# Attention with a fourth-power score and a mixture of experts: when relu buffers are given back, and a new set of order weights

## The chip, the cores and the metric

The kernel runs on one core of one Trainium2 chip. The metric is the time of one execution on the device in microseconds (us), the median over several executions. The core has five engines that work side by side, each through its own queue of instructions: TensorE (PE, matmuls; PEld is its weight loads), VectorE (DVE), ScalarE (ACT), GpSimd (POOL) and SyncE (SP, which here issues transfers). An engine takes the instructions of its queue in the order in which the program issued them.

## What is computed

A block over x of 4 batches, 1024 tokens and 128 channels. The normed input goes through an attention with 16 heads of 8 channels and through 8 experts of which each token takes 2; both results are added to x.

```python
xn = _layernorm(x)
# attention, per batch and head
s = einsum('td,sd->ts', q, k)
s = s - s.mean(-1); mad = abs(s).mean(-1) + 1e-6
s = where(causal, s / mad * score_gain, -1000.0)
r = maximum(s, 0.0) ** 4
att = r / (r.sum(-1) + 1e-6)
y = att @ v
# experts, per token, the two best of 8 with softmax weights
z = (xn @ w1[e] + b1[e]) * (xn @ w2[e] + b2[e])
out += weight * (silu(z @ wg[e] + bg[e]) @ w3[e] + b3[e])
x = x + attention + experts
```

The softmax is replaced by a relu to the fourth power, so a score is squared twice. The mean of the absolute scores is needed as well, over all tokens and not the causal ones alone.

## The kernel before

The program first describes its work as nodes and then has a planner put them in order. A node (`Plan.add`) has a name, the engines that could run it with a duration for each, the nodes that it depends on, the buffers that it takes and those that it gives back. `Plan.run` simulates the engines: again and again it looks at all nodes whose dependencies are met, and for each at every engine that could run it, computes the start that the engine and the buffers allow, and takes the node with the smallest key. The key is

```python
sooner = self.SOONER.get(n.name, 0.0) + self.SOONER.get(f"{n.name}@{e}", 0.0)
key = (s - sooner, n.rank + self.RANK.get(n.name, 0.0), s + took)
```

So `SOONER` holds a bonus in us for a name, and for a name on one engine; `RANK` only parts nodes whose first part of the key is equal. Instructions are then issued in order of the planned starts. That order is what each engine's queue has on the chip; waits between engines come from semaphores that follow the data, not from the planned times. Buffers are numbered slots of a kind, picked by the planner.

Attention is done in chunks: for each of 4 batches two chunks of 512 queries. Names carry a "0" in the first batch's two chunks (stage 0: `sq0`, `mask0`, `abs0` and so on) and a "2" in the last chunk. Heads come in 4 rounds (r) of 4, whose matmuls run in four quarters of the array at once. In a round:

- "up" (L1010) makes scores of queries against all keys that the causal part doesn't cover into 4 PSUM banks; "abs" sums their absolute values, on VectorE (L1023) or ScalarE (L1025), and gives the banks back.
- "score" (L1134) makes scores of a group of keys, transposed, into 4 banks. It also takes two relu buffers, `u1s`, of which there are 6 in all, enough for three groups.
- "mask" (L1153, VectorE) and "relu" (L1160 on ScalarE, L1162 on VectorE) move the scores into the relu buffers and free the banks.
- "sq" squares twice, on ScalarE (L1185) or POOL (L1187): the first squares (`sq1`) read the relu buffer and write a buffer `u`, the second (`e2`) work in place in `u`.
- "av" is a burst of two jobs (`flush`): the sums of relus (L1201, which read the relu buffers `u1`) and the values (L1210, which read `u`), both into one accumulator bank.
- "ys", "turn" (L1078) and "normal" evacuate, transpose and divide; "yT", "wT" and "proj" (L1267, L1269, L1279) project a whole chunk.

There are 8 PSUM banks for all of this. For each batch, "k", "q", "kappa", "bound", "keys", "blocks" and "heads" prepare the keys and queries.

Routing goes once over all batches: "top" finds the two best experts of each token, "count" and "place" (six nodes on VectorE, L663 to L703) give each token a slot in an expert's list, "weight" and "gates" the weights. Then POOL scatters the normed rows to their slots in DRAM with 64 indirect transfers ("scatter", L776). Before each eight of them "second" (L767) writes the weights into the rows. When all rows have been scattered, 36 tiles of experts run: "rows_in" and "load" (SP), "xg" (L1331), "h" (L1342, and L1360 of the tile before), "g" (L1351), "y", and "give" (L1380), an indirect transfer of POOL that adds the results in DRAM. At the end those sums are loaded back ("sums"), added on POOL ("sum", L1486) and stored.

The planner also pads: where TensorE would idle it adds matmuls with zeros (L1531, L1536).

Of the kernel before, what the change touches and what calls it, by code (L numbers as in the profile page):

```python
# [52 lines left out]
class Plan:  # L53
# [3 lines left out]
    HOP = 0.12  # L57
    LAG = {"PE": 0.2, "DVE": 0.085, "ACT": 0.1, "POOL": 0.045}

    SOONER = {"score": 0.46, "sum": -0.74, "mean": 0.17, "wT@DVE": 0.13, "norm@ACT": -0.05, "place": 0.03, "sums": 0.22, "relu0": -0.21, "relu2": -0.08, "score0": 0.74, "score2": 0.58, "sq2": 0.1, "ys0": -0.42, "out": -0.17, "v": -0.03, "gain": -0.81, "absq": 0.38, "abs0": -0.55, "sq0": -0.35, "proj": -0.44, "xT": 0.07, "second": -0.98, "up2": 0.18, "yT": 0.14, "up": 0.32, "sq@ACT": -0.27, "tbias": -0.01, "mask0": 0.04, "up0": 0.3, "abs0@DVE": 0.57, "ys2": -0.14, "ys@DVE": -0.79, "sq@POOL": -0.64, "weight": -0.19, "gate@ACT": -0.71, "count": 0.31, "k": 0.27, "turn": -0.06, "xT@ACT": 0.41, "y@DVE": 0.14, "gateT": 0.32, "abs2@DVE": 0.08, "gate": 0.05, "scatter": -0.07, "heads@ACT": 0.06, "abs@DVE": -0.3, "exp": 0.12, "xT@DVE": -0.16, "moments": -0.1, "keys": -0.69, "heads@DVE": 0.12, "relu0@ACT": -0.27, "rows": -0.52, "av0": -0.04, "scale": 0.09, "sq2@ACT": -0.42, "xg": -0.43, "av2": 0.03, "ys": 0.07, "abs2": 0.05, "warm": -0.75, "bias": -0.8, "gates": 0.91, "std": 0.14, "ys@ACT": -0.12, "sq0@ACT": -0.2, "q@ACT": 0.05, "ys2@ACT": -0.68, "mask": -0.04, "q": 0.08, "bound@DVE": -0.04, "norm": 0.17, "y": 0.11, "yT@DVE": -0.66, "norm@DVE": -0.66, "ys0@ACT": 0.07, "give": 0.2, "sq0@POOL": 0.01, "yT@ACT": -0.42, "headsT": 0.91, "abs2@ACT": -0.01, "blocks": -0.07, "sq": -0.1, "rows_in": -0.92, "xg@ACT": 0.35, "h": 0.17, "relu@DVE": -0.2, "load": 0.26, "xg@DVE": -0.07, "bound": 0.03, "abs": 0.51, "spill": -0.52, "kappa": 0.65, "relu2@DVE": -0.07, "relu": 0.05}  # L60
    RANK = {"xg": -16, "headsT": 6, "spill": 168, "blocks": 174, "wT": 8, "absq": 58, "abs": 20, "weight": 101, "gain": 188, "keys": -227, "abs2": 39, "sq2": 19, "ys0": -9, "up0": -37, "score2": 1, "av": -8, "second": 1, "score0": 14, "relu2": 94, "heads": -7, "norm": 28, "abs0": -107, "h": 174, "sums": 228, "av0": 17, "xT": -7, "relu": -11, "stats": -9, "rows_in": -149, "gateT": -21, "sq": 161, "top": 102, "reload": 84, "ys2": 27, "k": 242, "up": 10, "hot": -130, "score": -18, "sum": 13, "mean": 156, "kappa": -33, "load": -208, "warm": 37, "ys": -195, "yT": 1, "turn": -123, "rows": -17, "av2": 1, "out": 6, "normal": 62, "proj": -184, "scale": 29, "fill": 13, "mask2": 35, "sq0": -53, "tbias": -32, "count": 13, "gates": 7, "std": 24, "up2": -6, "gate": 6, "bias": 6, "mask0": -13, "v": 14, "scatter": 1, "g": 53, "moments": -184}
    MODE = {"up": "rows", "score": "rows", "av": "columns", "gate": "columns", "heads": "columns"}

    @classmethod
# [13 lines left out]
    def add(self, name, on, emit, deps=(), take=(), give=(), rank=0.0, after=0.0, begin=0.0,  # L78
            behind=()):
        n = Node(name, on, emit, deps, list(take), list(give), rank, after, begin, behind)  # L80
        self.nodes.append(n)
        return n

    def run(self):
# [9 lines left out]
        while len(order) < len(self.nodes):  # L94
            best = None
            for n in ready:
# [81 lines left out]
def layer_kernel(  # L178
# [63 lines left out]
    def keep(shape, name, dtype=F32):  # L242
        return const.tile(shape, dtype, name=name)
# [16 lines left out]
    add = plan.add  # L260
# [11 lines left out]
    rows = keep([3, P], "rows")  # L272
# [8 lines left out]
    gain = keep([P, 1], "gain")  # L281
# [14 lines left out]
    for r in range(NR):  # L296
        for g in range(4):
            h = g * NR + r
# [20 lines left out]
    for base, step in ((0, -D), (D - 1, D)):  # L319
        nc.gpsimd.affine_select(  # L320
            out=same.rearrange("p (h d) -> p h d", d=D), in_=same.rearrange("p (h d) -> p h d", d=D),
# [7 lines left out]
        out=causal[:, : 2 * P].rearrange("p (n k) -> p n k", k=P), in_=causal[:, : 2 * P].rearrange("p (n k) -> p n k", k=P),  # L329
# [3 lines left out]
    for i in range(kinds["V"][0]):  # L333
        v = keep([P, TB, VW], f"V_{i}")
# [11 lines left out]
        out=behind_, in_=behind_, compare_op=ALU.is_ge, fill=0.0,  # L346
# [53 lines left out]
    none = tiles["w"][0][:, FILL * WX : FILL * WX + 2 * C]  # L400
# [43 lines left out]
    hot = [keep([P, E, NTB], f"hot_{k}") for k in range(2)]  # L444
# [350 lines left out]
    q, km, Vb, sh, prepared, keyed = {}, {}, {}, {}, {}, {}  # L795
# [190 lines left out]
    def chunk(b, c, vd, sh_done, t0, t1):  # L986
# [10 lines left out]
        for n, (r, unit) in enumerate(work):  # L997
# [20 lines left out]
            for g, k in enumerate(ks_):  # L1018
                def drain(e, r=r, parts=parts, g=g, k=k):
                    for i, sg, _, w, at in parts:  # L1020
# [9 lines left out]
                        deps=[a], behind=drained[0][:1], take=[] if drained[0] else [asum], give=[k], rank=rank - 200,  # L1030
# [15 lines left out]
        def flush(jobs, rank):  # L1046

            n = add(
                "av" + stage, {"PE": sum(o["took"] for o in jobs)}, lambda e: [o["emit"](e) for o in jobs],
                deps=[d for o in jobs for d in o["deps"]] + chain, take=[t for o in jobs for t in o["take"]],  # L1050
                give=[u for o in jobs for u in o["give"]], rank=rank - 20,
                behind=line["turn"][-2:-1] if any(o["take"] for o in jobs) else [],
            )
            chain[:] = [n]
            for o in jobs:
                if o["last"]:
                    n.closed = o["acc"]
                else:
                    n.open = o["acc"]
            for o in jobs:  # L1060
                if o["free"]:
                    u1s, e2 = o["free"]
                    add("free", {"none": 0.0}, None, deps=[n] + e2, give=u1s)
                if o["last"]:
                    finish(*o["last"], n, rank)

# [46 lines left out]
        for r in range(NR):  # L1113
            acc = Buf("bank")
            for j, grp in enumerate(groups):
                diag = grp[0][0] >= c * CB
# [9 lines left out]
                e1, e2, sq1 = [], [], []  # L1126
                u1s, us = ([Buf(kind) for _ in range(2)] for kind in ("u1", "u"))
# [17 lines left out]
                for m in range(2):  # L1145
                    u1, u = u1s[m], us[m]
                    a = []
                    for g in range(2):
                        k = ks_[2 * m + g]
# [20 lines left out]
                        if rest:  # L1170
# [3 lines left out]
                                    give=[] if near else [k], rank=rank - 200,  # L1174
# [31 lines left out]
                def values(e, r=r, parts=parts, us=us, acc=acc, begin=False, end=False):  # L1206
# [11 lines left out]
                begin, last = j == 0, j == jn - 1  # L1218
                relu_job = dict(
                    acc=acc,  # L1220
                    emit=lambda e, f=relus, s=begin and not diag: f(e, begin=s), deps=e1, took=took(counted), give=[],
                    free=(u1s, e2), last=None, take=[acc] if begin and not diag else [],
                )
                av_job = dict(
                    acc=acc,
                    emit=lambda e, f=values, s=begin and diag, t=last: f(e, begin=s, end=t), deps=e2 + vd, took=took(w),
                    give=us, free=None, last=(r, acc) if last else None, take=[acc] if begin and diag else [],
                )
                if begin and diag:
# [17 lines left out]
        k, yT = Buf("bank"), Buf("yT")  # L1247
# [7 lines left out]
        kw, wT = Buf("bank"), Buf("wT")  # L1255
# [10 lines left out]
        def project(e):  # L1266
# [15 lines left out]
            deps=[a] + first, give=[ko], rank=rank - 200,  # L1282
# [246 lines left out]
    for n in plan.run():  # L1529
# [4 lines left out]
        if n.pad:  # L1534
            acc, count = n.pad
# [33 lines left out]
```

## Time and profile before

| What | Before |
|---|---|
| median of 14 runs | 896.28 us (895.79 to 898.2) |
| the profiled execution | 896.33 us, of which the span of instructions 894.6 us |
| granted TensorE clock | 0.997 |
| scatter (L776), first and last start | 73.2 and 242.9 us |
| squares on POOL (L1187) | 302, 524.0 us |
| squares on ScalarE (L1185) | 338, 325.1 us |
| sums of absolute values on VectorE (L1023) | 417, 203.3 us |
| the same on ScalarE (L1025) | 351, 170.7 us |
| relus on ScalarE (L1160) and VectorE (L1162) | 353, 152.7 us and 159, 99.3 us |

Times of one instruction are averages over the profiled execution. A busy engine is one that has an instruction in it; for TensorE this includes matmuls that are drawn long since they wait for the one ahead.

```profile
L1187 POOL TENSOR_TENSOR u<-u 128x1024 f32<-128x1024 f32 (+1 forms) x302 | 524.0, 1832 | 93.4 <-ACT u L1160 47.3
L1185 ACT ACTIVATE u<-u 128x1024 f32<-128x1024 f32 (+1 forms) x338 | 325.1, 992 | 7.4 <-DVE u L1162 3.1
```

These are two of the page's costliest groups: line, engine, operation, what is written and read with its shape, how many; then busy us and mean ns of one; then the engine's idle time before them and what ended most of it.

### The profile page before, as it was taken

How to read it: one execution, taken by the hardware profiler on the slowest of the kernel's cores; microseconds unless marked ns; L12 is line 12 of the kernel's file. 1: busy time of each engine (PE TensorE's matmuls, PEld its weight loads, DVE VectorE, ACT ScalarE, POOL GpSimd, SP SyncE). 2: the span in 40 equal slices, each digit the busy share in tenths (PEclk: the TensorE clock that was granted, in tenths of full speed). 3: DMA queues.
4: the chain of work that ended last, by engine and by line, in shares of the span. 5: the costliest groups of instructions: out<-in, count | busy, mean ns of one | idle time of the engine just before them, and what ended most of it. 6: DMA issues, size and time to landing. Idle time of an engine off the chain costs nothing.

```text
span 894.6 us, 22584 instructions
## 1 busy us (share of the span) xinstructions
PE 875.9 (98%) x8067; PEld 469.5 (52%) x8067; DVE 593.3 (66%) x1557; ACT 787.1 (88%) x1881; POOL 710.4 (79%) x563
## 2 busy tenths in 40 slices
PE   7999999999999999999999999999999999999997
PEld 5455433334555555555566665555545666544444
DVE  6998967687865655554666666555756775755555
ACT  4978999999996999899988989989988978889995
POOL 5378998999995978787667839889787568599998
PEclk9999999999999999999999999999999999999999
DMA  4852001000001454535444534444213444422115
GB/s 112 311 153 86 25 26 32 31 13 25 26 20 49 101 128 91 127 77 144 94 111 105 134 92 120 96 122 117 72 52 73 104 111 107 108 72 54 23 15 186
DMA packets 92318, 79.20 MB, mean 89 GB/s; under 512 B 8431, under 2 KB 88366, under 8 KB 92206
## 3 DMA queue, kind: packets, MB, share of 16 engines
q1 hardware_dynamic: 79064, 68.50, 26.1%
q0 software_dynamic: 12416, 8.99, 7.3%
q8 instruction: 64, 1.05, 0.5%
q10 hardware_dynamic: 726, 0.27, 0.1%
q14 instruction: 48, 0.39, 0.1%
HBM read 58.13 MB, written 19.60 MB: 87 GB/s over the span
## 4 chain that ended last, share of the span: by engine, by line
PE 79%; ACT 6%; POOL 6%; DVE 5%; issue 2%; DMA 0%; DVEq 0%; POOLq 0%; ACTq 0%
PE bank L1010 16%; PE bank L1134 14%; PE bank L1210 14%; PE bank L1201 10%; PE bank L1351 7%; PE bank L1342 7%; PE bank L1360 4%; POOL u L1187 3%; ACT u L1185 2%; POOL xs L776 2%; ACT u L1160 2%; PE bank L1078 1%; DVE u L1153 1%; DVE asum L1023 1%; PE bank L1531 1%
## 5 line engine op out<-in xcount | busy, mean ns | idle before, releaser
L1187 POOL TENSOR_TENSOR u<-u 128x1024 f32<-128x1024 f32 (+1 forms) x302 | 524.0, 1832 | 93.4 <-ACT u L1160 47.3
L1185 ACT ACTIVATE u<-u 128x1024 f32<-128x1024 f32 (+1 forms) x338 | 325.1, 992 | 7.4 <-DVE u L1162 3.1
L1023 DVE TENSOR_REDUCE asum<-bank 128x1 f32<-128x512 f32 (+3 forms) x417 | 203.3, 547 | 71.3 <-PE bank L1010 70.1
L1025 ACT ACTIVATE bank<-bank 128x512 f32<-128x512 f32 (+3 forms) x351 | 170.7, 488 | 33.8 <-PE bank L1010 31.0
L1010 PE MATMUL bank<-blk,blk 32*128 32x512 f32 (+3 forms) x1536 | 181.2, 521 | 1.6 <-ACT s L1452 1.6
L1160 ACT ACTIVATE u<-bank 128x256 f32<-128x256 f32 (+2 forms) x353 | 152.7, 496 | 34.1 <-PE bank L1134 17.8
L1134 PE MATMUL bank<-blk,blk 32*128 32x512 f32 (+3 forms) x1536 | 178.4, 525 | 1.2 <-ACT blk L908 0.7
L1153 DVE SCALAR_TENSOR_TENSOR u<-bank,causal 128x256 f32<-128x256 f32 (+1 forms) x384 | 121.2, 373 | 74.4 <-PE bank L1134 37.7
L1380 POOL DMA_INDIRECT acc<-ye,xg x72 | 113.4, 1575 | 67.5 <-DVE ye L1372 39.3
L1210 PE MATMUL bank<-u,V 128*32 128x512 f32 (+3 forms) x1536 | 159.2, 497 | 0.1
L1162 DVE TENSOR_SCALAR u<-bank 128x512 f32<-128x512 f32 (+1 forms) x159 | 99.3, 660 | 50.1 <-PE bank L1134 50.0
L1010 PEld LDWEIGHTS bank<-blk,blk 32*128 32x128 f32 x1536 | 86.1, 183 | 80.3 <-DVE asum L1023 14.0
L1201 PE MATMUL bank<-u,pick 128*32 128x512 f32 (+3 forms) x1280 | 125.4, 469 | 0.0
L1134 PEld LDWEIGHTS bank<-blk,blk 32*128 32x128 f32 x1536 | 65.6, 183 | 64.5 <-issue 25.6
L1201 PEld LDWEIGHTS bank<-u,pick 128*32 128x32 f32 x1280 | 42.3, 111 | 80.3 <-issue 75.6
L1210 PEld LDWEIGHTS bank<-u,V 128*32 128x32 f32 x1536 | 32.8, 108 | 88.3 <-issue 67.3
L1351 PEld LDWEIGHTS bank<-z,w 128*128 128x128 f32 x576 | 67.2, 192 | 18.4 <-issue 5.9
L1426 DVE SCALAR_TENSOR_TENSOR z<-bank,biases,z 128x128 f32<-128x128 f32 x144 | 43.6, 345 | 46.2 <-ACT z L1419 45.6
L776 POOL DMA_INDIRECT xs<-blk,slot x64 | 62.9, 982 | 13.4 <-issue 10.7
L1351 PE MATMUL bank<-z,w 128*128 128x128 f32 x576 | 73.3, 280 | 0.0
L1342 PE MATMUL bank<-xT,w 128*128 128x128 f32 x576 | 70.3, 275 | 0.0
L1025 ACT ACTIVATION_READ_ACCUMULATOR bank<-bank 128x1 f32 x351 | 68.3, 195 | 0.0
(191 smaller groups left out, 724.3 us busy)
## 6 DMA issues: line engine op xcount, KB each, us to landing
w<-in_L_ffn_w_dram SPq DMA_DIRECT2D x216, 128.0 KB
w<-in_L_ffn_wg_dram SPq DMA_DIRECT2D x72, 256.0 KB
xs<-w SPq DMA_DIRECT2D x1, 4680.0 KB
xg<-xs SPq DMA_DIRECT2D x36, 130.0 KB
acc<-w SPq DMA_DIRECT2D x1, 2048.0 KB
blk<-acc SPq DMA_DIRECT2D x4, 512.0 KB
out_dram<-xt SPq DMA_DIRECT2D x8, 256.0 KB
xt<-in_L_attn_x_dram SPq DMA_DIRECT2D x3, 512.0 KB
```

The costliest lines, as they stand in the source:

```text
L1010: nc.tensor.matmul(of_buf(ks_[g])[:, at : at + w], of_buf(q[b])[rows_, ii * P : (ii + 1) * P], of_buf(km[b][r])[rows_, k0 : k0 + w], start ...
L1023: nc.vector.tensor_reduce(to, of_, AX.X, ALU.add, apply_absolute_value=True)
L1025: nc.scalar.activation(of_, of_, AF.Abs, accum_out=to)
L1134: nc.tensor.matmul(of_buf(ks_[g])[:, at : at + n], of_buf(km[b][r])[rows_, jj * P : (jj + 1) * P], of_buf(q[b])[rows_, c * CH + off : (c + ...
L1153: nc.vector.scalar_tensor_tensor(of_buf(u1)[:, g, :near], of_buf(k)[:, :near], 0.0, allowed[:, :near], ALU.max, ALU.mult)
L1160: nc.scalar.activation(to, s_, AF.Relu)
L1185: nc.scalar.activation(to, s_, AF.Square)
L1187: (nc.vector if e == "DVE" else nc.gpsimd).tensor_tensor(to, s_, s_, ALU.mult)
L1201: nc.tensor.matmul(of_buf(acc)[32 * g : 32 * g + 32, off + lo : CH], pick, of_buf(u1s[g // 2])[:, g % 2, at + lo : at + n], start=begin, s ...
L1210: nc.tensor.matmul(of_buf(acc)[32 * g : 32 * g + 32, off:CH], of_buf(Vb[b])[:, jj, h0 : h0 + 32], of_buf(us[g // 2])[:, g % 2, at : at + n ...
L1342: nc.tensor.matmul(of_buf(k)[:, m * TW + j * TS : m * TW + (j + 1) * TS], weights_of(i, j)[m][:, f * P : (f + 1) * P], of_buf(tile_[i]["xT ...
L1351: nc.tensor.matmul(of_buf(k)[:, g * TW + j * TS : g * TW + (j + 1) * TS], weights_of(i, j)[2][:, f, g * P : (g + 1) * P], of_buf(tile_[i][ ...
```

## The change

Two things. The relu buffers of a group are given back, in the plan, once the sums of relus and the first squares of the group are done, where before it was the sums of relus and the second squares. And both tables of weights for the order, `SOONER` and `RANK`, are replaced.

```diff
             for o in jobs:
                 if o["free"]:
-                    u1s, e2 = o["free"]
-                    add("free", {"none": 0.0}, None, deps=[n] + e2, give=u1s)
+                    u1s, squared = o["free"]
+                    add("free", {"none": 0.0}, None, deps=[n] + squared, give=u1s)
...
-                    free=(u1s, e2), last=None, take=[acc] if begin and not diag else [],
+                    free=(u1s, sq1), last=None, take=[acc] if begin and not diag else [],
...
                     if not counted:
-                        add("free", {"none": 0.0}, None, deps=e2, give=u1s)
+                        add("free", {"none": 0.0}, None, deps=sq1, give=u1s)
```

Of the tables, the bonuses of the names that the text speaks of, in us; on an engine the bonus of the name and that of the name on the engine add up, and what is not in the table is 0:

| Node, engine | before | after |
|---|---|---|
| score, up, av on PE | 0.46, 0.32, 0 | 0.41, 0.06, -0.20 |
| second, scatter on POOL | -0.98, -0.07 | 0.75, -0.18 |
| sq0 on POOL, on ACT | -0.34, -0.55 | 0, 0.01 |
| sq on POOL, on ACT | -0.74, -0.37 | -0.79, -0.48 |
| place, mask0, abs0 on DVE | 0.03, 0.04, 0.02 | -0.66, 0, 0.05 |
| mask on DVE | -0.04 | 0.66 |
| relu on DVE, on ACT | -0.15, 0.05 | 0.63, -0.01 |
| abs on DVE, on ACT | 0.21, 0.51 | 0, 0.10 |
| give on POOL | 0.20 | -0.12 |

More of the change, by code (lines that the diff above doesn't have):

```diff
@@ L58 @@
     LAG = {"PE": 0.2, "DVE": 0.085, "ACT": 0.1, "POOL": 0.045}
-    SOONER = {"score": 0.46, "sum": -0.74, "mean": 0.17, "wT@DVE": 0.13, "norm@ACT": -0.05, "place": 0.03, "sums": 0.22, "relu0": -0.21, "relu2": -0.08, "score0": 0.74, "score2": 0.58, "sq2": 0.1, "ys0": -0.42, "out": -0.17, "v": -0.03, "gain": -0.81, "absq": 0.38, "abs0": -0.55, "sq0": -0.35, "proj": -0.44, "xT": 0.07, "second": -0.98, "up2": 0.18, "yT": 0.14, "up": 0.32, "sq@ACT": -0.27, "tbias": -0.01, "mask0": 0.04, "up0": 0.3, "abs0@DVE": 0.57, "ys2": -0.14, "ys@DVE": -0.79, "sq@POOL": -0.64, "weight": -0.19, "gate@ACT": -0.71, "count": 0.31, "k": 0.27, "turn": -0.06, "xT@ACT": 0.41, "y@DVE": 0.14, "gateT": 0.32, "abs2@DVE": 0.08, "gate": 0.05, "scatter": -0.07, "heads@ACT": 0.06, "abs@DVE": -0.3, "exp": 0.12, "xT@DVE": -0.16, "moments": -0.1, "keys": -0.69, "heads@DVE": 0.12, "relu0@ACT": -0.27, "rows": -0.52, "av0": -0.04, "scale": 0.09, "sq2@ACT": -0.42, "xg": -0.43, "av2": 0.03, "ys": 0.07, "abs2": 0.05, "warm": -0.75, "bias": -0.8, "gates": 0.91, "std": 0.14, "ys@ACT": -0.12, "sq0@ACT": -0.2, "q@ACT": 0.05, "ys2@ACT": -0.68, "mask": -0.04, "q": 0.08, "bound@DVE": -0.04, "norm": 0.17, "y": 0.11, "yT@DVE": -0.66, "norm@DVE": -0.66, "ys0@ACT": 0.07, "give": 0.2, "sq0@POOL": 0.01, "yT@ACT": -0.42, "headsT": 0.91, "abs2@ACT": -0.01, "blocks": -0.07, "sq": -0.1, "rows_in": -0.92, "xg@ACT": 0.35, "h": 0.17, "relu@DVE": -0.2, "load": 0.26, "xg@DVE": -0.07, "bound": 0.03, "abs": 0.51, "spill": -0.52, "kappa": 0.65, "relu2@DVE": -0.07, "relu": 0.05}
@@ L61 @@
-    RANK = {"xg": -16, "headsT": 6, "spill": 168, "blocks": 174, "wT": 8, "absq": 58, "abs": 20, "weight": 101, "gain": 188, "keys": -227, "abs2": 39, "sq2": 19, "ys0": -9, "up0": -37, "score2": 1, "av": -8, "second": 1, "score0": 14, "relu2": 94, "heads": -7, "norm": 28, "abs0": -107, "h": 174, "sums": 228, "av0": 17, "xT": -7, "relu": -11, "stats": -9, "rows_in": -149, "gateT": -21, "sq": 161, "top": 102, "reload": 84, "ys2": 27, "k": 242, "up": 10, "hot": -130, "score": -18, "sum": 13, "mean": 156, "kappa": -33, "load": -208, "warm": 37, "ys": -195, "yT": 1, "turn": -123, "rows": -17, "av2": 1, "out": 6, "normal": 62, "proj": -184, "scale": 29, "fill": 13, "mask2": 35, "sq0": -53, "tbias": -32, "count": 13, "gates": 7, "std": 24, "up2": -6, "gate": 6, "bias": 6, "mask0": -13, "v": 14, "scatter": 1, "g": 53, "moments": -184}
+    SOONER = {"score": 0.41, "sum": -0.51, "mean": -1.23, "wT@DVE": 0.99, "norm@ACT": 0.12, "place": -0.66, "sums": 0.17, "gate@DVE": 0.09, "relu2": 0.33, "score0": 0.51, "score2": 0.47, "sq2": -0.62, "ys0": -0.74, "v": -0.26, "gain": 0.49, "absq": -0.12, "abs0": 0.05, "proj": -0.53, "xT": 0.08, "second": 0.75, "up2": 0.09, "yT": -0.55, "bound@ACT": 0.29, "relu@ACT": 0.14, "up": 0.06, "relu0@DVE": -0.5, "sq@ACT": -0.23, "tbias": 0.18, "up0": 0.49, "ys2": 0.2, "ys@DVE": 0.59, "sq@POOL": -0.54, "weight": 0.38, "gate@ACT": -0.35, "count": 0.4, "hot": 0.76, "k": 0.39, "turn": -0.14, "xT@ACT": 0.3, "fill": -0.49, "y@DVE": 0.62, "gateT": 0.03, "abs2@DVE": -0.61, "gate": -0.02, "scatter": -0.18, "heads@ACT": -0.17, "exp": 0.13, "moments": -0.51, "keys": -0.46, "heads@DVE": -0.08, "rows": 1.24, "av0": -0.17, "g": -0.13, "top": 0.31, "wT": -0.12, "scale": 0.35, "sq2@ACT": 0.16, "xg": -0.17, "av2": -0.1, "ys": -0.38, "abs2": 1, "warm": -0.06, "normal": -0.04, "heads": -0.22, "std": 0.18, "ys@ACT": 0.37, "sq0@ACT": 0.01, "q@ACT": -1.78, "ys2@ACT": 0.5, "abs0@ACT": 0.04, "mask": 0.66, "q": 0.07, "bound@DVE": 0.76, "yT@DVE": 0.13, "norm@DVE": -0.32, "ys0@ACT": 1.68, "give": -0.12, "blocks": -1.24, "abs@ACT": 0.1, "sq2@POOL": 0.26, "relu": -0.15, "yT@ACT": -0.1, "abs2@ACT": -0.69, "relu2@ACT": -0.05, "load": 0.31, "rows_in": 1.06, "ys2@DVE": 0.42, "xg@ACT": 0.02, "relu2@DVE": -0.13, "av": -0.2, "bound": -0.14, "relu@DVE": 0.78, "kappa": 0.42, "h": 0.02, "spill": 0.26, "sq": -0.25}
@@ new lines @@
+    RANK = {"xg": -15, "headsT": 25, "spill": 10, "blocks": -9, "y": 188, "exp": -1, "abs": 15, "weight": -238, "keys": 23, "abs2": 27, "relu0": -28, "sq2": 20, "ys0": -28, "up0": 66, "score2": -20, "av": -242, "second": 2, "score0": 11, "relu2": -156, "heads": -79, "place": -25, "norm": -9, "abs0": 24, "h": -14, "sums": -92, "av0": -11, "xT": 26, "rows_in": 7, "q": -2, "bound": -1, "sq": 21, "top": -71, "ys2": -97, "k": -11, "up": -16, "hot": -1, "score": -19, "sum": -28, "mean": 87, "kappa": -6, "give": 192, "load": 22, "ys": 17, "yT": 223, "turn": 34, "rows": -7, "av2": 227, "mask": -188, "out": 130, "scale": 4, "fill": 23, "mask2": -181, "sq0": -37, "bias": -154, "up2": 199, "mask0": 7, "scatter": 13, "moments": 140, "tbias": -20, "g": -14, "count": 44, "v": 14, "std": -70, "gates": 72}
```

## The prediction

> **What bounds the kernel now.** I read the page first: busy times, then the chain.
>
> ```profile
> span 894.6 us, 22584 instructions
> PE 875.9 (98%) x8067; PEld 469.5 (52%) x8067; DVE 593.3 (66%) x1557; ACT 787.1 (88%) x1881; POOL 710.4 (79%) x563
> PE 79%; ACT 6%; POOL 6%; DVE 5%; issue 2%; DMA 0%; DVEq 0%; POOLq 0%; ACTq 0%
> ```
>
> The reader is to see that TensorE leads, but also that its 98% can't be streaming: a matmul that waits is drawn long. So I looked for the rate at which it streams when nothing stops it, in the chain in order of time:
>
> ```profile
> 415.85 0.86 PE bank L1201 x8
> ...
> 433.18 1.09 PE bank L1360 x8
> 434.27 1.79 PE bank L1342 x16
> ```
>
> Eight records of 512 columns of the packed form (four quarters of the array at once) take 0.86 us, sixteen of 128 columns of the full form 1.79 us, 0.11 each. Counting every matmul record of the trace at these rates gives 713 us of streaming in a span of 894.6. By stretches (my count, from the records): 0 to 64 us 40.2 of 64; 64 to 245 us 137.6 of 181, a share of 0.76; 245 to 300 us 0.73; 300 to 850 us 461.4 of 550, 0.84; 850 to 895 us 0.74. The kind of matmul changes 0.98 times per us in 300 to 850, and a change costs 0.11 us (median over 93 changes from L1134 to L1210, start to start less the streaming), so there only some 0.05 of the time, 28 us, is real waiting. The slack lies in the first 300 us. Busy times by window say why:
>
> ```profile
> core 0: us, PE busy (x) PEld busy (x) DVE busy (x) ACT busy (x) POOL busy (x), PEclk, DMA share, GB/s
> ...
> 110.00:150.00 40.00, 40.00 (x353) 13.99 (x353) 27.88 (x68) 37.24 (x69) 36.35 (x48) 1.00 0.08 26
> ...
> 300.00:400.00 100.00, 100.00 (x931) 55.03 (x934) 56.51 (x149) 91.42 (x225) 81.51 (x49) 1.00 0.46 109
> ```
>
> From 110 to 150 us ScalarE is 93% busy and POOL 91%: attention runs alone there, its squares fill both, and TensorE waits for them. From 300 us the experts, which are mostly TensorE, run beside it. They begin when the last of 64 scatters has left POOL. POOL's timeline shows what those scatters wait for:
>
> ```profile
> 185.13 21.66 POOL L1187 TENSOR_TENSOR u<-u 128x1024 f32<-128x1024 f32 x12
> 206.73 0.20 POOL L767 COPY blk<-pr 128x8 f32<-128x8 f32 x1
> ...
> 219.02 14.50 POOL L1187 TENSOR_TENSOR u<-u 128x512 f32<-128x512 f32 x10
> 233.47 0.20 POOL L767 COPY blk<-pr 128x8 f32<-128x8 f32 x1
> ...
> 242.94 0.97 POOL L776 DMA_INDIRECT xs<-blk,slot  x1 [0.21 <-issue]
> ```
>
> L767 is the step "second", 0.2 us, which opens a group of eight scatters. Squares were put in ahead of it six times: 8.7, 9.8, 7.4, 6.9, 21.7 and 14.5 us by the same timeline, 69 us in all. The last waits I read are those for banks:
>
> ```profile
> PEld bank L1010 <- DVE asum L1023: 14.0, 40, 0.8
> ...
> PEld bank L1134 <- DVE asum L1023: 9.5, 16, 0.8
> ...
> PEld bank L1078 <- DVE asum L1023: 6.4, 9, 0.8
> ```
>
> TensorE's weight loads wait 30 us for VectorE's sums of absolute values to empty a bank. None lasts over 0.8 us, about one burst, so most of it lies under a matmul still streaming.
>
> **The change, part by part.** No instruction of the attention, the routing or the experts is added or taken away; durations of one stay. What can change is the order on each engine, which engine takes a node that has two, and the padding matmuls (24 of L1536 and 62 of L1531, 20 us busy now, in waits).
>
> *Buffers given back sooner.* The second squares read and write "u", not the relu buffer, so the chip never had to wait for them; only the plan did. How often did that bind? I set the start of each of the 160 score bursts against the end of the square whose buffers it needs in the plan (three groups back). The median distance is 6.6 us; 3 of 157 bursts start within 0.6 us, 8 within 1.7 us, the three all between 160 and 225 us. So the edit alone is worth 0 to 8 x 1.7 x (1 - 0.77) = 3 us. I take -0.5, near the three.
>
> *The new order.* The plan takes the node with the smallest start less its bonus (SOONER by name plus by name and engine, in us). RANK only parts nodes that tie. So I compared bonuses on one engine.
>
> (a) POOL, first 245 us: "second" goes from -0.98 to +0.75, squares of stage 0 from -0.34 to 0. Then "second" was passed over, now it goes first. Against that, "scatter" goes from -0.07 (0.27 ahead of squares) to -0.18 (0.18 behind): the 64 scatters, 1.27 us apart when back to back, now yield to ready squares. All 69 us regained would put the last scatter at 174 us; yielding could also leave it 30 us later than now (the sum of the two longest waits of "second", 36 us, less a bit). I take 35 us sooner, half of the best. A microsecond sooner turns one at 0.77 streaming into one at 0.84: 0.065 us. So -2.3, between -4.5 and +2. The squares passed over are not lost: ScalarE and POOL have them later, when POOL is 73 to 82% busy. If that cover is gone, all of the 2.3 is.
>
> (b) VectorE, routing: "place" goes from 0.03, level with masks and sums of stage 0, to -0.66, behind both (0 and 0.05). Its six nodes run now from 48.8 to 59.3 us in a VectorE that is 93% busy (23.26 of 25 us). Queued behind them are "tbias", "weight", "second", all scatters and so the experts. If each waits for one more mask or sum pair (1.3 us), 8 us; if as "second" did, 20 us or more. I take 11 us, at the same 0.065: +0.7, between 0 and +2.
>
> (c) VectorE and ScalarE, after stage 0: relu on VectorE goes from -0.15 to +0.63, on ScalarE from 0.05 to -0.01. Now ScalarE has 353 relus, 152.7 us, and VectorE 159, 99.3 us. If a quarter of the 353 moves, ScalarE loses 38 us, 5% of its 787, and VectorE gains 88 x 0.69 at most, 60 us, to 73%. ScalarE's 6% of the chain is 54 us; 5% of that is -2.6. The bound on one side is twice that, -5.
>
> (d) On VectorE masks and relus (0.66, 0.63) now go ahead of the sums of absolute values (0); before the sums led (0.21 against -0.04 and -0.15). Squares get fed sooner, banks of "up" come free later. This is the other bound of (c): 160 up bursts, 0.6 of them meeting a busy VectorE, 0.69 us each, 66 us of later banks, of which TensorE's unstreamed share of 0.16 shows: +10.6. I take none of it in the sum, as the waits above never outlast a burst; it is the rival below.
>
> Sum: -0.5 - 2.3 + 0.7 - 2.6 = -4.7. The profiled execution took 896.33 us (span 894.6 and 1.7 around it), the median of 14 runs is 896.28, so nothing need be scaled: 891.6.
>
> A rule of the Trainium skill ("Perfetto Trace Analysis", section "Optimizing Scalar/DVE Operations") speaks against (c): VectorE and GpSimd share a read port, so moving work towards VectorE may cost GpSimd what it saves. The trace doesn't show it: large POOL squares have a median of 1.895 us where over 1 us of relu (L1162) overlaps them (22 cases) and the same where none does (164). By the rule 60 us of held POOL at its 6% of the chain would be +3.6 and the sum 897.8; I go by the row.
>
> **The rivals.** *Slower: banks late.* Place: VectorE from 245 us on, L1023 behind L1153 and L1162. For it: the bonus turns by 0.85 us in all, eight banks serve up, score, accumulator and experts, and 30 us of weight loads wait there already. Against: no such wait outlasts a burst. It decides from the point where a sum waits longer than the 0.8 us that a streaming burst covers. Without the gains of (c): 896.3 + 10.6 - 2.1 (the rest of the sum) = 905.
>
> *No change.* Experts start sooner but end under the same TensorE, which streams 713 us in any order; what the first 300 us gain is given back at the end, where sums and stores (L1486, 10 us on POOL at the end of the span) must follow the last scatter-add. The edit to the buffers, which binds in 2% of bursts, is all that is left: 895.8.
>
> *It doesn't do what it says.* The buffers come back sooner in the plan only, and the new order was drawn up for plan durations; where the chip's waits differ, as with the scatters that yield, experts begin 30 us later and routing 11: +2 + 0.7 and no gain elsewhere: 899.
>
> **How the numbers follow.** Forecast 891.6: 0.48. Banks late, 905: 0.28. Experts later, 899: 0.16. No change: 0.08. The first is the likeliest. Differences under 0.2%, 1.8 us, can't be told from none here. Faster 0.48, same 0.08, slower 0.44. The forecast's own range is 884 (all bounds of a to c, -3 - 4.5 - 5 = -12.5) to 894; with the others it reaches up to 908, banks late with none of the gains and routing later (896.3 + 10.6 + 0.7).
>
> **What would show it.** (a) L767 follows the scatter before it with no run of squares between, and L1342 begins before 245 us (267 now). (b) L691 later than 56.8 us. (c) fewer than 353 relus on ScalarE, its busy time under 787. (d) the wait of L1010 and L1134 for L1023 over 24 us. Buffers: score bursts closer after the squares than 6.6 us. The prediction is wrong if experts begin later than now with ScalarE as busy, or if the share of streaming from 300 to 850 us falls under 0.84.

## The result, and the profile after

The changed kernel takes 904.73 us (median of 6 runs, 904.33 to 905.07), the kernel before 896.35 beside it: 1.0088 of before [1.0078, 1.0097]. It is slower by 8 us where 4.7 were to be gained. The profiled execution has a span of 902.4 us, against 894.6.

Page of the changed kernel: busy times, the chain's shares, the groups that moved.

```profile
span 902.4 us, 22568 instructions
PE 879.8 (97%) x8081; PEld 473.2 (52%) x8081; DVE 624.8 (69%) x1617; ACT 784.5 (87%) x1885; POOL 678.8 (75%) x543
PE 83%; ACT 6%; DVE 4%; POOL 3%; issue 1%; DMA 1%; POOLq 0%; ACTq 0%; DVEq 0%; SPq 0%
...
L1185 ACT ACTIVATE u<-u 128x1024 f32<-128x1024 f32 (+1 forms) x358 | 340.6, 981 | 20.1 <-DVE u L1162 13.1
...
L1025 ACT ACTIVATE bank<-bank 128x512 f32<-128x512 f32 (+3 forms) x395 | 188.8, 479 | 28.1 <-PE bank L1010 24.9
L1162 DVE TENSOR_SCALAR u<-bank 128x512 f32<-128x512 f32 (+2 forms) x247 | 142.4, 618 | 66.4 <-PE bank L1134 65.1
...
L1160 ACT ACTIVATE u<-bank 128x512 f32<-128x512 f32 (+2 forms) x265 | 116.2, 492 | 35.9 <-PE bank L1134 17.5
```

88 relus went from ScalarE (353 to 265, 36.5 us) to VectorE, as forecast. But ScalarE took 44 sums of absolute values (18.1 us) and 20 squares (15.5 us) in exchange, and its busy time fell by 2.6 us (787.1 to 784.5), not by 38. VectorE gained 31.5 us, POOL lost 31.6.

Where the 7.8 us of span lie comes from the prediction's own count of streaming, without the padding matmuls: 699.6 us in every program here, so the time at which the 300th, 400th and 600th of them is issued can be set side by side. This is worked out from the matmul records, in us of the span. The experiments that the later columns belong to follow below.

| Piece of the work | before | after | e1: before's order | e2: before's order, then the new | e3: the new, then before's | e12: relu engines | e17: after again |
|---|---|---|---|---|---|---|---|
| start to 300th | 412.3 | 411.6 | 441.2 | 440.9 | 473.9 | 441.9 | 472.2 |
| 300th to 400th | 119.6 | 124.7 | 119.7 | 124.5 | 119.6 | 121.5 | 124.5 |
| 400th to 600th | 239.3 | 241.8 | 239.2 | 242.9 | 239.3 | 239.7 | 242.2 |
| 600th to last matmul | 118.6 | 117.2 | 118.6 | 117.3 | 118.5 | 118.7 | 117.3 |
| last matmul to the end | 4.8 | 7.1 | 4.9 | 6.6 | 4.9 | 4.8 | 7.0 |

The first two columns: -0.7, +5.1, +2.5, -1.4, +2.3. The first 412 us, on which most of the prediction's working was spent, come out even (with 6.8 us at half TensorE clock in them, 3.4 before). Five are lost between 412 and 536 us, where attention and experts run side by side, and two at the end.

From the 300th us of streaming to the last matmul, the time in which TensorE does not stream (start to start of two matmuls, less the streaming of the first, by the same count) grew from 77.9 to 84.1 us. Of these 6.2 us, 3.9 stand ahead of one line, the experts' L1360 ("h"): 10.5 before, 14.4 after. In the stretch of the five its part is 1.4; the rest is spread over many lines there. This view of the line lists what weight loads and matmuls of L1360 sat idle for, in us and times over the whole span. First before, then after:

```profile
  issue: 6.0, 10
  ACT u L1185: 3.8, 5
  ACT bank L1025: 1.7, 4
  DVE u L1153: 1.6, 3
  ACT s L1452: 1.3, 3
...
  DVE u L1162: 0.8, 1
```

```profile
  DVE u L1162: 7.2, 10
  issue: 5.9, 10
  ACT u L1160: 3.7, 4
  DVE u L1153: 2.3, 4
...
```

The releasers L1153, L1160 and L1162 are the masks and relus that empty a score burst's four banks. Before, they held it up 4 times, 2.4 us; after, 18 times, 13.2 us. Part of it lies under a matmul still streaming, and part stands in place of other waits: all that the view lists for the line went from 16.8 to 24.3 us. The chain of waits of the changed kernel, in order of time, shows one such place:

```profile
484.80 1.11 PE bank L1134 x8
485.90 0.28 DVE u L1153
486.21 0.88 ACT u L1160 x2
487.18 0.49 DVE u L1153 x2
487.67 0.94 DVE u L1162 x2
488.66 1.16 PE bank L1360 x8
```

A score burst ends, masks and relus of its banks alternate between VectorE and ScalarE for 2.7 us, and only then has the experts' burst its bank. Of 36 such bursts, 6 started more than 0.5 us after the matmul ahead had streamed, against 2 before.

The same kind of view of the end:

```profile
880.74 3.35 DMA acc<-ye,xg
...
884.14 4.06 DMA blk<-acc
...
888.27 6.18 POOL xt L1486 x5
894.45 1.22 POOLq L1564
895.67 2.44 POOL xt L1486 x2
```

The last scatter-add lands, the sums are loaded, POOL adds them. Before, the last scatter-add was issued at 867.7 us and the loads of the sums from 870.9 on. POOL then still had squares to do until 880.3; its additions ran from there to 890.3, as the last projection on TensorE ended (890.1), and the addition behind it (L1279) waited for the projection. Now the scatter-add is issued at 880.7, the additions cannot start before 888.3, and they end the kernel.

Fourteen of the eighteen experiments (all but e5 to e8) came under another condition: in their sets of runs the kernel before took 924 to 926 us, not 896, with nothing in it changed, and TensorE was at half speed for some 34 us of its order instead of 3.4 (e1, whose program is that of before). Pieces of these runs are read against e1's. Each ratio below is to before in the same set; the section on the hardware comes back to it.

### The profile page after: what moved, and what is told of

The parts are those of the page before. It is cut to its first block, busy times and chain, and to the rows that moved or that the text cites. A ratio compares the mean times of both kernels' runs of the same rounds, so it can differ in the third digit from the quotient of the medians.

```text
span 902.4 us, 22568 instructions
## 1 busy us (share of the span) xinstructions
PE 879.8 (97%) x8081; PEld 473.2 (52%) x8081; DVE 624.8 (69%) x1617; ACT 784.5 (87%) x1885; POOL 678.8 (75%) x543
## 4 chain that ended last, share of the span: by engine, by line
PE 83%; ACT 6%; DVE 4%; POOL 3%; issue 1%; DMA 1%; POOLq 0%; ACTq 0%; DVEq 0%; SPq 0%
PE bank L1010 17%; PE bank L1134 15%; PE bank L1210 14%; PE bank L1201 10%; PE bank L1351 7%; PE bank L1342 7%; PE bank L1360 4%; ACT u L1185 2%; POOL u L1187 2%; PE bank L1078 2%; ACT u L1160 2%; DVE u L1153 2%; PE bank L826 1%; ACT bank L1025 1%; POOL xt L1486 1%
## 5 line engine op out<-in xcount | busy, mean ns | idle before, releaser
L1187 POOL TENSOR_TENSOR u<-u 128x1024 f32<-128x1024 f32 (+1 forms) x282 | 486.7, 1793 | 139.1 <-DVE u L1162 77.8
L1185 ACT ACTIVATE u<-u 128x1024 f32<-128x1024 f32 (+1 forms) x358 | 340.6, 981 | 20.1 <-DVE u L1162 13.1
L1023 DVE TENSOR_REDUCE asum<-bank 128x1 f32<-128x512 f32 (+3 forms) x373 | 185.9, 552 | 46.6 <-PE bank L1010 45.8
L1025 ACT ACTIVATE bank<-bank 128x512 f32<-128x512 f32 (+3 forms) x395 | 188.8, 479 | 28.1 <-PE bank L1010 24.9
L1162 DVE TENSOR_SCALAR u<-bank 128x512 f32<-128x512 f32 (+2 forms) x247 | 142.4, 618 | 66.4 <-PE bank L1134 65.1
L1010 PE MATMUL bank<-blk,blk 32*128 32x512 f32 (+3 forms) x1536 | 183.7, 528 | 0.5 <-ACT bank L1025 0.2
L1134 PE MATMUL bank<-blk,blk 32*128 32x512 f32 (+3 forms) x1536 | 178.8, 527 | 0.9 <-DVE blk L876 0.8
L1153 DVE SCALAR_TENSOR_TENSOR u<-bank,causal 128x256 f32<-128x256 f32 (+1 forms) x384 | 121.7, 373 | 82.5 <-PE bank L1134 60.9
L1160 ACT ACTIVATE u<-bank 128x512 f32<-128x512 f32 (+2 forms) x265 | 116.2, 492 | 35.9 <-PE bank L1134 17.5
L1010 PEld LDWEIGHTS bank<-blk,blk 32*128 32x128 f32 x1536 | 88.5, 185 | 77.9 <-DVE asum L1023 15.4
L1134 PEld LDWEIGHTS bank<-blk,blk 32*128 32x128 f32 x1536 | 66.8, 184 | 61.3 <-issue 21.6
L1025 ACT ACTIVATION_READ_ACCUMULATOR bank<-bank 128x1 f32 x395 | 75.2, 190 | 0.0
L776 POOL DMA_INDIRECT xs<-blk,slot x64 | 61.9, 968 | 14.5 <-issue 12.5
L1342 PE MATMUL bank<-xT,w 128*128 128x128 f32 x576 | 70.3, 275 | 0.0
L1342 PEld LDWEIGHTS bank<-xT,w 128*128 128x128 f32 x576 | 67.2, 192 | 0.8 <-ACT bank L1025 0.8
```

Source lines behind the costliest of these rows:

```text
L1010: nc.tensor.matmul(of_buf(ks_[g])[:, at : at + w], of_buf(q[b])[rows_, ii * P : (ii + 1) * P], of_buf(km[b][r])[rows_, k0 : k0 + w], start ...
L1023: nc.vector.tensor_reduce(to, of_, AX.X, ALU.add, apply_absolute_value=True)
L1025: nc.scalar.activation(of_, of_, AF.Abs, accum_out=to)
L1134: nc.tensor.matmul(of_buf(ks_[g])[:, at : at + n], of_buf(km[b][r])[rows_, jj * P : (jj + 1) * P], of_buf(q[b])[rows_, c * CH + off : (c + ...
L1153: nc.vector.scalar_tensor_tensor(of_buf(u1)[:, g, :near], of_buf(k)[:, :near], 0.0, allowed[:, :near], ALU.max, ALU.mult)
L1162: nc.vector.tensor_scalar(to, s_, 0.0, None, ALU.max)
```

## The experiments

**The give-back alone (e1).** The order and engines of before are written out as a list; only the give-back is new.

```diff
-    SOONER = {...}
+    SEQ = "P1 D1 P1 D1 D5 A-4 ..."
...
-        while len(order) < len(self.nodes):
+        for at_, e in self.sequence():
...
-                    free=(u1s, e2), last=None, take=[acc] if begin and not diag else [],
+                    free=(u1s, sq1), last=None, take=[acc] if begin and not diag else [],
```

> The relu buffers are given back as in the changed kernel, but the order and the engine of every node are those of before, written out as a list. The plan's own end is 892.2 us, that of before (the new order's is 896.1). If the loss comes from the new order, the time is that of before: 896.4 us, within 0.3. If the earlier give-back itself costs something (a buffer taken again sooner, a wait for its last reader), 898 us or more.

Measured: 925.7 us, before 925.0; 1.0002 [0.9981, 1.0023]. With the order held, the program is instruction for instruction that of before, so the new give-back can act through the planner's order alone. The old tables with the new give-back, planned afresh, were not run.

**Half an order each (e2, e3).** Both with the new give-back. e2 takes the order of before for nodes planned in the first 300 us and the new one after; e3 the other way round.

```diff
-    SEQ = "<all of before>"
+    SEQ = "<one order for nodes planned before 300 us, the rest in the other>"
```

> The order of before for all nodes that its plan starts before 300 us, then the new order for the rest; nothing is left out. The plan's own end is 896.1 us, exactly that of the new order. Theory 'late order' (the loss arises after 300 us: TensorE does not stream for 92.9 us between 300 and 850 in the changed kernel, 88.6 before, and its end comes later): 903 to 905 us. Theory 'early order' (routing, scatters and the start of the experts, all of which are as before in this run): 896 to 898 us.

> The other way round: the new order for all nodes that its plan starts before 300 us, then the order of before. The plan's own end is 898.9 us, since the joint costs something. Late order: 898 to 901 us, better than the changed kernel although its plan is 2.8 us longer. Early order: 904 to 908 us.

Measured: e2 935.44 us, 1.0113 [1.0075, 1.0152], and once more 935.13, 1.0103 [1.0062, 1.0144] (e10). e3 958.1, 1.0356 [1.0328, 1.0385]. The table above reads them: with the new order late (e2) the piece from the 300th to the 400th us takes 124.5 us and the end 6.6; with before's order late (e3) 119.6 and 4.9, as in before. So the loss that the result shows goes with the late order, under both conditions, and L1360's waits for masks and relus go with it (13.2 us in e2 too). What e3 loses lies in the first piece, 33 us, and is of another kind (last section); by its time alone, which neither expectation covers, it would have spoken for the early order.

**Relu engines alone (e12).** Order of before, but 288 relus run on the engines that the new order gives them.

```diff
-    (in words) relu, engine of before, at its place in SEQ
+    (in words) relu, engine of the new order, at the same place
```

> The order of before, but the 288 relus between the first and the last stage run on the engine that the new order gives them: 131 on VectorE in place of 73; squares and sums of absolute values stay on their engines. The prediction's step: ScalarE is relieved of relus, and a quarter of all relus moved brings 2.6 us: 895 us here. Rival: in an order that was fitted to the other engines VectorE becomes late for the squares; the plan's end is 900.6 us, and with the 4.2 us that before takes over its plan: 904 to 908 us.

Measured: 928.78 us, before 925.36; 1.0044 [1.0027, 1.0061]. Its groups of relus:

```profile
L1162 DVE TENSOR_SCALAR u<-bank 128x512 f32<-128x512 f32 (+2 forms) x217 | 129.7, 627 | 57.6 <-PE bank L1134 54.1
...
L1160 ACT ACTIVATE u<-bank 128x256 f32<-128x256 f32 (+2 forms) x295 | 129.9, 497 | 38.1 <-PE bank L1134 17.5
```

58 relus moved, ScalarE was relieved by them (788.0 us busy in e1, 768.8 here) with nothing put in their place, and the kernel got slower, by less than either size expected: 1.8 of its 3.0 us of span in the same piece as the changed kernel's five. At one width, 128x512, a relu takes 685 ns on VectorE and 601 on ScalarE. In before's order, then, the prediction's step (c) had the wrong sign. But that order was made for the other engines, and the loss has another place than the changed kernel's: 2.5 us more unstreamed time ahead of score bursts (L1134), 0.2 ahead of L1360. What the moved relus cost in an order of their own was not measured.

**The end (e8, e16).** The changed kernel, and then the kernel before, without the two scatter-adds of the last tile of experts; those rows are missing in the output.

```diff
                 def give(e, j=j):
+                    if i == n_ - 1:
+                        return
                     nc.gpsimd.indirect_dma_start(
```

> The changed kernel without the two scatter-adds of the last expert tile; the results of that tile's rows are left out of the output. The order is the same. In the changed kernel's trace the last projection's addition waits 2.96 us for POOL's sums, which wait for the last scatter-add. If that end costs what the trace says, 1.2 us or a little more is gained against the changed kernel. If TensorE's end sets the time, nothing is gained.

> The kernel before without the two scatter-adds of the last tile of experts (their rows are missing in the output), the counterpart of the same cut in the changed kernel, which took 2.7 us off it. In before the last sums are loaded at 870.9 us and the last TensorE burst ends at 888.9 whatever they do: within 0.1% of before (0 to 0.9 us off) if the chain through the last scatter-add ends only the changed kernel; 2 us off or more if it stands on both kernels' end, and then it explains nothing of the difference.

Measured: e8 901.43 us, 1.0049 [1.003, 1.0068], against 904.1, 1.008 [1.006, 1.0099], for the changed kernel beside it (e5). So 2.7 us hang on them; last matmul to end fell from 7.1 to 4.4 us. In before the same cut gave nothing, though that was measured where before takes 925: e16 1.0016 [0.9999, 1.0032]. These 2.7 us belong to the change, as far as the two conditions can be compared.

**Experts sooner (e4, e9, e15).** Tables of before, new give-back, and one weight of the new table.

```diff
-    "second": -0.98
+    "second": 0.75
```

> The tables of before with one name changed: 'second' gets the new bonus of 0.75; with the new give-back. In its plan the last scatter starts at 188 us in place of 242 and the first rows of the experts are fetched at 200 in place of 254, while the plan's end is 897.9 us, 5.7 later than before. By the prediction's price of 0.065 us for each us that the experts start sooner: 896.4 - 3.5 = 893 us. If experts that start sooner are worth nothing by themselves and the time follows the plan's end (896.4 is 4.2 over the plan of before, 904.7 is 8.7 over the plan of the change): 902 to 906 us.

> The kernel before with the new give-back and the one weight 'second' of 0.75: plan end 897.85, experts planned 54 us sooner. It took 0.991 of before where before runs at half speed for 36 us. If its gain is only that TensorE stays at full speed early on, it takes 897.85 + 4 to 6 = 902 to 904 us on a chip where before takes 896 (ratio 1.006 to 1.009), and again 0.991 where before takes 925. If the sooner experts themselves are worth something, it is at or under before on both kinds of chip.

Measured: 916.91, 914.71 and 914.17 us; 0.9906 [0.9877, 0.9935], 0.9911 [0.9876, 0.9947] and 0.9901 [0.9877, 0.9925]. The scatters end at 203 us (263 in e1) and L1342 begins at 256.5 (296.8). In e15 the first 300 us of streaming are issued at 423.6 us, 17.6 sooner than in e1, with TensorE at half speed for 6.8 us instead of 34. After that it loses 6.8 us against e1. Whether it is faster where before takes 896 was not measured.

**Place (e11).** The changed kernel with before's weight for the routing steps.

```diff
-    "place": -0.66
+    "place": 0.03
```

> The changed kernel with the bonus that 'place' had before (0.03 in place of -0.66). In the plan the last of its nodes starts at 73.8 us in place of 79.9, the first rows of the experts are fetched at the same time and the end is the same, 896.1. The prediction gave the later routing 0.7 us. If routing that is late is hidden behind the scatters: 904 us, the changed kernel's time.

Measured: 966.92 us, 1.0444 [1.0412, 1.0476], no better than the changed kernel in such a set (e17). L691 starts at 75.0 us, against 78.0. The weight that the prediction blamed moves the routing by 3 of some 20 us; the rest must come from the other weights.

**Padding against half speed (e6, e7).** Before and the changed kernel with more matmuls with zeros ahead of work: 59 instead of 31, and 70 instead of 36.

```diff
-            if open_ and idle > 0.3:
+            if open_ and idle > 0.22:
...
-            elif then.bank and then.start < 100.0:
+            elif then.bank and then.start < 330.0:
```

> The kernel before with more padding matmuls in the planned idle time of the first 330 us (59 ahead of bursts in place of 31; the order is the same). If half-speed stretches in the first 310 us are what separates chips, they become fewer and the time comes down: on a chip where before takes 925 us to 905 or less, where it takes 896 to 893 to 896. If padding only stands in the way, 0 to 4 us longer.

> The same for the changed kernel (70 in place of 36). If the clock carries the loss, it comes within 4 us (the difference of the two plans' ends, 3.9) of the padded kernel before. If waits after 300 us carry it, it stays 8 us behind it.

Measured: e6 897.11, 1.0007 [0.9995, 1.0018]; e7 908.56, 1.0139 [1.0113, 1.0165], 4.5 us over the changed kernel, with the same 6.8 us at half speed. Padding does not help here; where before takes 925 it was not run.

**Orders from a longer search (e13, e18, e14).** New tables, found by minimising the end of the kernel's own plan: e13 with the old give-back, plan end 886.99 us (before 892.16), e14 with the new one, 891.83 (after 896.06).

```diff
-    SOONER = {...}
-    RANK = {...}
+    SOONER = {... 887 us by the plan}
+    RANK = {...}
```

> The kernel before (old give-back), with tables from a longer search; its plan ends at 886.99 us where that of before ends at 892.16. Theory 'the plan's end carries over': 5 us faster than before, ratio 0.994 (891 us where before takes 896, 920 where before takes 925). Rival 'what the chip adds to a plan differs by as much as the plans do': the ratio lies anywhere from 0.985 to 1.03 and the sum of half-speed stretches of TensorE, or the lag of the last bursts behind the plan, differs from before's by over 5 us.

> The changed kernel (new give-back) with tables from the same search, grown from the changed kernel's own; its plan ends at 891.83 us where the changed kernel's ends at 896.06 and before's at 892.16. Theory 'the order alone costs, the new give-back nothing, and the plan's end carries over': within 0.4% of before (896 to 900 us where before takes 896, and 4 us under the changed kernel there). Rival 'the new give-back is what costs': 0.8% slower than before whatever the plan says. Rival 'what the chip adds differs by as much': anything else, with half-speed stretches or a lag behind the plan that show it.

> The kernel before with the searched tables (plan end 886.99 against 892.16), which took 0.9835 of before where before takes 925. Where before takes 896 and TensorE hardly runs at half speed: 889 to 893 us (ratio 0.992 to 0.997) if the plan's end carries over; 894 to 900 if the gain was only that TensorE stayed at full speed for longer. Where before takes 925: 0.9835 again.

Measured: e13 908.54, 0.9835 [0.9817, 0.9854], and e18 909.68, 0.9841 [0.9807, 0.9875], the fastest of all where before takes 925. e14 963.65, 1.043 [1.0411, 1.0449], though its plan is 4 us shorter than the changed kernel's. The plan's end does not carry over under this condition: e13's gain of 15 us of span against e1 lies wholly in the first 300 us of streaming (425.2 against 441.2), and after them it takes 483.4 us, e1 482.4. Neither was run where before takes 896, so a version that beats both kernels is shown for the one condition only.

**The changed kernel where before takes 925 (e17).** No edit.

> The changed kernel as it is. Where before takes 925 us: the runs that share its order up to 300 us took 958 and 967 there with 78 to 82 us at half speed, so 955 to 970 us (ratio 1.033 to 1.05) if that order's first 300 us are what brings the half speed on, and about 933 (925 + 8, ratio 1.009) if the change costs the same 8 us whatever the chip does. Where before takes 896: 904 again.

Measured: 964.55 us, 1.0432 [1.0407, 1.0457]. By the table, 31 us of it lie before the 300th us of streaming, and 8.6 after (491.0 against 482.4 in e1), the same loss as in the result (490.8 against 482.3).

## Why the prediction was wrong

*What bounds it.* The reading of the bound stands: the same 699.6 us of streaming, TensorE first. The inference "the slack lies in the first 300 us" is what misled: there the two kernels come out even, and it was in the fuller part, at a share of 0.84, that 6 us could still be lost.

*Buffers, -0.5.* Zero with the order held (e1); what the edit does to a plan made afresh is not known. The trace of the changed kernel shows no gain: score bursts follow the needed squares by 6.8 us in the median after, 6.6 before.

*(a) -2.3, experts 35 us sooner.* The first half came true, the second not. POOL's timeline after:

```profile
102.39 0.20 POOL L767 COPY blk<-pr 128x8 f32<-128x8 f32 x1 [0.21 <-DMA xs<-blk,slot]
...
136.60 33.26 POOL L1187 TENSOR_TENSOR u<-u 128x1024 f32<-128x1024 f32 x19 [0.18 <-ACT u L1160]
169.79 0.09 POOL L775 MEMSET scrap<- 1x1 f32 x1
170.04 0.99 POOL L776 DMA_INDIRECT xs<-blk,slot  x1 [0.16 <-issue]
171.06 7.56 POOL L1187 TENSOR_TENSOR u<-u 128x1024 f32<-128x1024 f32 x4
```

L767 now follows a scatter directly, but single scatters wait behind squares for 33 us: the weight of "scatter" fell below the squares', the loss that the prediction had bounded and set at half of the gain. The last scatter starts at 252.8 us (242.9), L1342 at 271.8 (267.9). The start to the 300th us changed by -0.7 all the same.

*(b) +0.7, routing 11 us later.* L691 moved by 21 us (56.8 to 77.8). With (a): -1.6 forecast, -0.7 measured. Small either way. (The price of 0.065 should have been 0.07, 0.84 less 0.77; nothing hangs on it.)

*(c) -2.6, ScalarE relieved.* **This is the step that failed**, together with (d), of which none was taken. The term stood at -2.6 us for 38 us off ScalarE. In the changed kernel ScalarE was relieved by 2.6 us only, since other steps with a choice of engine moved in; and where 58 relus did leave it (e12) the kernel lost 0.44%. A relu was priced by the time that it takes off an engine's total, but TensorE sees it where it hands back a bank. There the runs show a loss: from the 300th us of streaming on, the unstreamed time of TensorE ahead of matmuls whose start or weight load a mask or relu released grew from 13.0 to 19.6 us, while all of it grew by 6.2.

*(d) and the rival "banks late", 905.* It has the right number, in part by luck, and half of the mechanism. The engines at the place were VectorE and ScalarE with masks and relus, from 300 us on. But the banks that came late were not those of the sums of absolute values: L1010 and L1134 wait 24.1 us for them (23.5 before), and no such wait is over 0.8. The waits of the changed kernel's weight loads show which did:

```profile
PEld bank L1010 <- DVE u L1162: 10.3, 15, 0.8
...
PEld bank L1134 <- DVE asum L1023: 8.7, 14, 0.8
...
PEld bank L1360 <- DVE u L1162: 5.9, 7, 1.1
```

These are us in total, times and the longest. The last, of L1360, was 0.8 us in 1 before. The first was 2.3 us in 8, but there ScalarE's relus (L1160) fell from 13.3 to 2.5 us, so the relus of both engines hold L1010 for less than before, 12.8 us against 15.6; it is L1360 that waits longer. The size, 10.6, was worked out for the other path, and measured is 6.2 from the 300th us to the last matmul; 905 came out because the end, which was in no sum, added 2.3. The 6.2 are shown to go with the late order (e2, e3). That late masks and relus cause most of it is read from the traces and not shown by a run of its own: e12 moved relus alone and lost elsewhere. How it splits among the weights is open too: one weight changed moves hundreds of nodes.

*The end* was in no sum. "No change" named it as the place where gains are given back; 2.7 us of the loss are there (e8), since the last scatter-adds run 13 us later.

*The prediction's own tests.* Experts began later (271.8 us against 267.9), with ScalarE nearly as busy (784.5 against 787.1), and the share of streaming from 300 to 850 us fell from 0.839 to 0.831: both signs that it named for being wrong came true.

## What to carry to other kernels

Price a step that moves between engines by who waits for its result, and not only by the busy time that it leaves: 58 relus, which hand back PSUM banks, cost 0.44% when they left the busier engine, in an order that was not made for it. A list scheduler refills an engine that is relieved, and its weights can't be priced one at a time; read the orders against each other, piece by piece at equal work done, and the piece that differs shows itself. Look at the end apart: loads issued 19 us before the last matmul cost nothing here, and loads issued 11 us before it ended the kernel.

## What the runs showed of the hardware

The same program ran at two levels: before took 896 us in the set of the result and in that of e5 to e8, and 924 to 926 in four others (medians; single runs 921 to 927). The granted clock was 0.997 and 0.98, and the difference arises in the first 285 us. Half speed is a part of it, some 78 us in e17 and e3, which share the new early order, and 31 to 34 in e1 and e2. It cannot be all: at half speed TensorE loses at most half of the time, and e1, with 30.7 us more of it than before, is 28.9 us longer. Set side by side matmul by matmul, e1 falls behind before in four places, and 13 of these us are lost there ahead of the half-speed stretches, at full clock. Each place begins in a run of six or eight scatters (L776) that POOL issues one behind the other.

In such runs, hand-overs between engines came late. Here are the 32 matmuls of one round of "up", in the changed kernel where before takes 896, and in e17:

```profile
218.36 4.51 PE L1010 MATMUL bank<-blk,blk 32*128 32x512 f32 x32
```

```profile
244.72 1.12 PE L1010 MATMUL bank<-blk,blk 32*128 32x512 f32 x2
252.14 2.07 PE L1010 MATMUL bank<-blk,blk 32*128 32x512 f32 x2 [6.31 <-issue]
258.46 2.07 PE L1010 MATMUL bank<-blk,blk 32*128 32x512 f32 x4 [4.25 <-DVE asum L1023]
264.17 2.77 PE L1010 MATMUL bank<-blk,blk 32*128 32x512 f32 x6 [3.64 <-issue]
276.83 4.85 PE L1010 MATMUL bank<-blk,blk 32*128 32x512 f32 x18 [9.89 <-DVE asum L1023]
```

They take 4.5 us there and 37 here, and half speed begins at 247.9, after TensorE has gone idle. VectorE's sum at 276.1 waits 11.3 us, ended by a signal that the profile assigns to no instruction ("remote"). Such waits stand in the profiles of all fourteen runs of the slower level, and in none of the six of the other. The more scatters follow each other in runs of six or more (starts less than 2.4 us apart), the longer the span: 908 to 917 us with 14 or 16, 923 to 933 with 28, 956 to 966 with 51 to 55. At the other level 28 to 51 bring no such wait. So the scatters go with the loss, but no run shows that they cause it, nor how.

Half speed lasts on in work that streams elsewhere. Windows of the profile, engines' busy time with the number of instructions, then clock, for e17:

```profile
core 0: us, PE busy (x) PEld busy (x) DVE busy (x) ACT busy (x) POOL busy (x), PEclk, DMA share, GB/s
...
101.10:128.40 27.30, 22.10 (x69) 11.41 (x73) 10.32 (x19) 10.50 (x36) 13.92 (x29) 0.50 0.10 34
```

and for the changed kernel where before takes 896:

```profile
100.00:115.00 15.00, 15.00 (x130) 9.52 (x130) 14.35 (x38) 14.34 (x58) 10.42 (x20) 1.00 0.16 50
```

The same work, score bursts for the sums of absolute values in a row, keeps TensorE at full speed in one and at half for 27.3 us in the other, in which it falls 20 us behind. The Trainium skill ("TensorE: Matmul & The Clock Gate", section "What's actually happening") has half speed as the default, released by a busy window of 3.41 us and restored by an idle one. The records agree in the two values and in the length: the stretches last 3.4, 6.8, 10.2, 27.3 and 37.5 us, 1, 2, 3, 8 and 11 windows. What no run here explains is the 27.3 us, in which TensorE has a matmul in it for 22.1 and is not released, nor what delays the signals and sets the level of a set of runs.
